# A two-layer graph network kernel: a seventh product split once more, additions begun from their addend, and one list schedule for every engine

## The chip, the cores and the metric

The kernel runs on one core of a Trainium2 chip. The metric is device time in microseconds (us), from the first to the last instruction of the core; the kernel before takes 1877.09 us, the median of three runs (1876.88 to 1878.52). A core has a matrix engine (TensorE, "PE" in the profile, with its weight loads as "PEld"), three engines for elementwise work (VectorE "DVE", ScalarE "ACT", GpSimd "POOL") and a queue of transfers (SyncE "SP"). Matmul results are in PSUM, eight banks of 128 x 512 float32; all else is in SBUF. Each engine works through its own list of instructions in the listed order and waits on semaphores for the others.

## The reference, cut to what matters

64 graphs of 256 nodes with 512 features, all float32. Two layers, each with a residual and a layer norm:

```python
# layer 0
deg = jnp.sum(adj, axis=-1, keepdims=True)
agg = jnp.einsum('bij,bjf->bif', adj, x) / jnp.maximum(deg, EPS)
out = relu(jnp.einsum('bnf,of->bno', jnp.concatenate([x, agg], axis=2), W))
x   = layernorm(x + out)
# layer 1
q, k = jnp.split(x @ Wqk, 2, axis=-1);  v = x @ Wv
agg  = jnp.einsum('bij,bjd->bid', adj, k * mask[:, :, None])
w    = inv_scale * mask * jnp.einsum('bid,bid->bi', q, agg)
x    = layernorm(x + softmax(w, axis=1)[:, :, None] * v)
```

The kernel moves matrices around the sums. In layer 0 it multiplies x with both halves of W first and lets adj act on the second result. In layer 1 it forms Wq Wk^T once, so that one product of x with [Wq Wk^T, Wv] (512 x 1024) gives what q and k give, and adj acts on x. So each layer of each graph is one 256 x 512 by 512 x 1024 product and one 256 x 256 by 256 x 512 product.

## The kernel before: the parts that count here

It works on **pairs** of graphs, 32 of them, and on layer 0 of pair j and layer 1 of pair j-1 in one round of its loop, so that each has work for TensorE while the other waits.

**The large product by Strassen (Winograd's form).** Both sides are cut into 2 x 2 blocks; seven block products P1 to P7 take the place of eight. Of these, P1, P2, P3 and P5 are cut once more and done by seven matmuls with 256 columns in place of eight. P4, P6 and P7 are done plainly, by four matmuls with 512 columns each for a pair.

```python
def inner(p, X, sides, w, q, done=lambda fifth: None):     # second step: 7 matmuls of 256 columns
    lo, hi = w[:, :HF], w[:, HF:]                          # two halves of a scratch bank
    def first_two():
        mm(hi, s(0), b["T1"], start=True)
        mm(lo, X.chunk(block, 0, 0), b["B11"])
        act.copy(q[0][:, :HF], lo)
        tick()
    def second():
        mm(lo, s(1), b["T2"])
        act.copy(q[0][:, HF:], lo)
        tick()
    def third():
        mm(lo, s(2), b["T3"])
        act.copy(q[1] ..., lo ... broadcast twice)         # cut
        fifth.append(small.tile([P, HF], F32, name="fifth", bufs=3))
        act.copy(fifth[0], hi)
        mm(q[0][:, :HF], X.chunk(block, 0, 1), b["B21"])
        tick()
    def last_two():
        mm(q[1][:, :HF], X.chunk(block, 1, 1), b["T4"])
        mm(q[0][:, HF:], s(3), b["B22"])
        if p in ("P1", "P5"):
            for k in range(2):
                vec.tensor_add(q[k][:, HF:], q[k][:, HF:], fifth[0])
        done(fifth[0])
        tick()

def outer(ps, k, X, slot, b, done=None):                   # plain: mm(ps[k], X.chunk(slot, k, e), b[:, e]), 512 columns
    ...
def pairs(ps, X, slot, b, done):
    return outer(ps, 0, X, slot, b, done) + outer(ps, 1, X, slot, b, done)
```

`s(r)` are sums of blocks of the left side ("xT_i", "x1T_i" in the profile; the outer sums are "xT_s", "x1T_s"), formed on GpSimd for every pair; the sums of the weights ("t", "t_i") are formed once, at the start. `q` are the two banks in which a product is accumulated onto the one before it; P6, P7 and P4 continue on P1's banks `u`.

**What happens to a finished product (layer 0; layer 1 is alike).**

```python
def after_p1(fifth):  act.copy(own[:, k, 0], u[k])                      # for k in 0, 1
def after_p2(fifth):  vec.tensor_add(own[:, k, 0], o[k], own[:, k, 0])  # for k in 0, 1
                      add_fifth(own[:, :, 0, HF:], fifth)
def after_p6(k):      act.copy(yt[:, k, 0], u[k]);  vec.tensor_add(yt[:, k, 0], y[k], yt[:, k, 0])
def after_p7(k):      act.copy(yt[:, k, 1], u[k]);  vec.tensor_add(yt[:, k, 1], y[k], yt[:, k, 1])
def after_p3(fifth):  vec.tensor_add(yt[:, k, 0], y[k], yt[:, k, 0])    # for k in 0, 1
                      add_fifth(yt[:, :, 0, HF:], fifth)
def after_p4(k):      act.copy(own[:, k, 1], u[k])
```

**The product with adj** (`gather`): seven matmuls of 256 columns for each graph, with adj's sums "sa" and the right side's sums "tv". In layer 0 the right half of the result goes into a tile `z`, and `norm0` adds z / deg to `own` later.

```python
def norm0(j):
    def scaled(k, t):
        vec.scalar_tensor_tensor(own[:, k, t, HF:], z[:, k, t], rdeg[:, k, t:t + 1], ..., op0=OP.mult, op1=OP.add)
    def residual(k, t, total):
        vec.scalar_tensor_tensor(o, o, 0.0, xs[j][:, k, t], op0=OP.max, op1=OP.add, accum_out=...)
```

**The order.** Every DVE, ACT and POOL instruction is issued through `InOrder.do`, which keeps program order (so the profile shows its line, L90, for nearly all of them), and every matmul through `mm` (L175). The side work that no product depends on at once (norms, masks, degrees, softmax) stands in queues; `tick()`, called after each step of a product, takes a step of a queue when a rough clock says that the engine is free. The order of the products is written by hand, in strings such as

```python
run("m p p", ...); fourth_sums(X, [0]); run("m p p m", ...); run("q q q", q=q); run("r q r m", ...); run("r s r", r=r, s=s)
run("s s j s a b", ...)                                    # s: P4 of layer 0; a to g: the product with adj
run("a n b q d q n c q e q n p g f", n=n, q=q, p=p, **g); b8(); run("p l p l p l", p=p, l=open1)
```

Of the kernel before, what the change touches and what calls it, by code (L numbers as in the profile page):

```python
# [2 lines left out]

# [6 lines left out]
F32 = mybir.dt.float32  # L36
# [5 lines left out]
P = 128  # L42
Q = 32
# [6 lines left out]

class Side:

    def __init__(self, pool, name, over, home=None):
        self.pool, self.name = pool, name
        self.slot = (0, 1, 2, over)
        home = pool.tile([P, 2 * N_SIDE], F32, name=name) if home is None else home
        self.a = home.rearrange("p (k u e v n) -> p k u e v n", k=2, u=2, e=2, v=2)
        self.s = self.i = None  # L60

    def open_sums(self):
        self.s = self.pool.tile([P, 2, 3, 2, P], F32, name=self.name + "_s")
        self.i = self.pool.tile([P, 4, 3, P], F32, name=self.name + "_i")

    def block(self, s, ks):
        return self.s[:, ks, self.slot[s]] if isinstance(s, int) else self.a[:, ks, s[0], :, s[1]]

    def chunk(self, s, k, e):
        return self.s[:, k, self.slot[s], e] if isinstance(s, int) else self.a[:, k, s[0], e, s[1]]  # L70

    def first_row(self, k, e):

        return self.a[:, k, :, e, 0]


class InOrder:

    def __init__(self, tc, engine, clock, cost):
        self.tc, self.engine, self.clock, self.cost, self.free = tc, engine, clock, cost, 0.0

    def __getattr__(self, name):
        def do(out, *args, **kwargs):
            size = 1
            for n in out.shape[1:]:
                size *= n
            self.free = max(self.free, self.clock[0]) + self.cost(name, size)
            return self.tc.keep_in_program_order(getattr(self.engine, name)(out, *args, **kwargs))  # L90
        return do
# [3 lines left out]
def resnorm_kernel(  # L95
# [22 lines left out]
    const = ctx.enter_context(tc.tile_pool(name="const", bufs=1))  # L118
    pool = ctx.enter_context(tc.tile_pool(name="pool", bufs=1))
    small = ctx.enter_context(tc.tile_pool(name="small", bufs=4))  # L120
    psum = ctx.enter_context(tc.tile_pool(name="psum", bufs=1, space=bass.MemoryType.PSUM))
    dram = ctx.enter_context(tc.tile_pool(name="dram", bufs=2, space=bass.MemoryType.DRAM))
    banks = [[psum.tile([P, F], F32, name=f"bank{2 * n + k}") for k in range(2)] for n in range(4)]

    (adjs, rows, xs, Xs, rdegs, sumsA, sumsM, owns, ys, zs, aggs, vs, x1Ts, scores, columns, rows_d, rows_w,
     probs) = ({} for _ in range(18))

    clock, chains, shared, quiet = [0.0], [], [1.0], [False]  # L130
    vec = InOrder(tc, nc.vector, clock, lambda name, n: shared[0] * ((0.17 if name == "bn_stats" else 0.07) + n / 960))
    act = InOrder(tc, nc.scalar, clock,
                  lambda name, n: 0.07 + n / 1200 if name == "copy" else (0.3 if n == F else 0.2) + n / 1000)
    gp = InOrder(tc, nc.gpsimd, clock, lambda name, n: 0.0)
    room = {vec: 0.6, act: 0.6}

    def queue(rank, name, *steps, ready=0.0):

        chains.append((rank, name, [ready], deque(steps)))
        chains.sort(key=lambda c: c[0])  # L140

    steady = []

    def step(chain):
        _, name, ready, steps = chain
        eng, work = steps.popleft()
        work()
        ready[0] = eng.free + (0.4 if eng is not vec else 0.7 if name == "norm" and len(steps) == NT else 2.2 if name == "finish" or name == "norm" and steady else 1.4) if steps and steps[0][0] is not eng else 0.0
        if not steps:
            chains.remove(chain)  # L150

    def tick():
        while not quiet[0]:
            for c in list(chains):
                if c[2][0] <= clock[0] and c[3][0][0].free <= clock[0] + room[c[3][0][0]]:
                    step(c)
                    break
            else:
                return

    def flush(*names):
        while True:
            c = next((c for c in chains if not names or c[1] in names), None)
            if not c:
                return
            step(c)

    def run(order, **units):
        for name in order.split():
            units[name].pop(0)()  # L170

    places, late_sums = [None], []

    def mm(ps, a, b, start=False):
        tc.keep_in_program_order(nc.tensor.matmul(ps, a, b, start=start, stop=True, skip_group_check=True))  # L175
        clock[0] += 0.86 if ps.shape[-1] == F else 0.43

    def first(out, in_):

        return tc.keep_in_program_order(nc.sync.dma_start(out, in_))  # L180

    send = first

    def load_adj(j):
        adjs[j] = pool.tile([P, 2, NT, N], F32, name="adj", bufs=2)
        for k in range(2):
            first(adjs[j][:, k], adj_t[2 * j + k].rearrange("(t p) i -> p t i", p=P))

    def load_rows(j):
        rows[j] = pool.tile([P, 2 * NT * F], F32, name="turn")[:, :2 * NT * N].rearrange(
            "p (k t n) -> p k t n", k=2, t=NT)
        for k in range(2):
            first(rows[j][:, k], adj[2 * j + k].rearrange("(t p) j -> p t j", p=P))

    def load_x(j):
        xs[j] = pool.tile([P, 2, NT, F], F32, name="x")
        for k in range(2):
            first(xs[j][:, k], x[2 * j + k].rearrange("(t p) f -> p t f", p=P))  # L200

    def load_xT(j, home=None):
        Xs[j] = Side(pool, "xT", S1, home)
        for k in range(2):
            first(Xs[j].a[:, k].rearrange("p h e t n -> p (h e) (t n)"),
                   x_t[2 * j + k].rearrange("(c p) n -> p c n", p=P))


    w0 = const.tile([P, 2 * NF, F], F32, name="w0")
    w1 = const.tile([P, 2 * NF, F], F32, name="w1")  # L210
    setup = ExitStack()
    sp = setup.enter_context(tc.tile_pool(name="setup", bufs=1))
    wqk = sp.tile([P, 2 * NA, F], F32, name="wqk")
    for a in range(NA):
        src = wqk_t.rearrange("(h a p) f -> a p h f", p=P, h=2)[a]
        first(wqk.rearrange("p (h a) f -> a p h f", h=2)[a], src)
    w0_of = w_t.rearrange("(k h p) o -> k p h o", p=P, h=H)
    for k in (0, 2):
        first(w0[:, k * H:(k + 1) * H, :], w0_of[k])
    load_xT(0)  # L220
    for k in (3, 1):
        first(w0[:, k * H:(k + 1) * H, :], w0_of[k])
# [3 lines left out]
    mask_sb = const.tile([P, B, NT], F32, name="mask_sb")  # L226
    first(mask_sb, mask_t)
    first(w1[:, NF:, :], wv.rearrange("(c p) o -> p c o", p=P))

    ident = const.tile([P, P], F32, name="ident")  # L230
    make_identity(nc, ident)
    eps = const.tile([P, 1], F32, name="eps")
    vec.memset(eps, LN_EPS)
    wide = [const.tile([P, Q], F32, name=f"wide{k}") for k in (0, 1)]
    for w in wide:
        vec.memset(w, 0.0)
    ones = const.tile([P, P], BF16, name="ones")
    vec.memset(ones, 1.0)

    def fill(pair):  # L240
        for k in range(2):
            mm(pair[k].rearrange("p (a n) -> p a n", n=P), ones,
               ones[:, None, :].to_broadcast([P, F // P, P]), start=True)
    for pair in (banks[0], *banks):
        fill(pair)

    def weight_product(c, ps):

        def unit(a):
            def go():  # L250
                mm(ps, wqk[:, a, c * P:(c + 1) * P], wqk[:, NA + a, :], start=(a == 0))
                if a == NA - 1:
                    act.copy(w1[:, c, :], ps)
                tick()
            return go
        return [unit(a) for a in range(NA)]

    def weight_sums(w, name):


        b11, b21, b12, b22 = (w[:, k * H:(k + 1) * H, :] for k in range(4))
        t1, t2, t4 = (const.tile([P, H, F], F32, name=f"{name}{k}") for k in (1, 2, 4))
        it = const.tile([P, 3, 4, HF], F32, name=f"{name}i")
        sides = {"T2": t2, "T3": b12, "T4": t4}
        sub = lambda *args: lambda: vec.tensor_sub(*args)

        def inner_of(n, p, b):
            c11, c12, c21, c22 = (b[:, e, h * HF:(h + 1) * HF] for e in range(2) for h in range(2))
            i1, i2, i4 = (it[:, r, n] for r in range(3))
            sides[p] = {"B11": c11, "B21": c21, "B22": c22, "T3": c12, "T1": i1, "T2": i2, "T4": i4}  # L270
            return [sub(i1, c12, c11), sub(i2, c22, i1), sub(c12, c22, c12), sub(i4, c21, i2)]
        work = ([sub(t1, b12, b11)] + inner_of(0, "P1", b11) + [sub(t2, b22, t1)] + inner_of(2, "P5", t1)
# [763 lines left out]
```

## Time and profile before

| What | Value |
|---|---|
| time, median of three | 1877.09 us |
| span of the profiled execution | 1877.0 us |
| PE busy, by its records | 1859.8 us in 7004 instructions |
| DVE, ACT, POOL busy | 1509.8, 1308.6, 910.1 us |
| mean granted TensorE clock | 0.998 |
| DMA, mean of the span | 97 GB/s, queue q1 35.8% of 16 engines |

How to read it: busy time is the time in which an engine worked on at least one instruction. Every float32 matmul stands in the trace as two records, and consecutive records overlap, so neither the sum of their lengths nor the busy share says how close TensorE is to its limit; the distance from one start to the next does. An idle stretch of an engine is put down to what it waited for ("released by"). The chain of waits follows the last instruction back, at each step to what released it.

### The profile page before, as it was taken

How to read it: one execution, taken by the hardware profiler on the slowest of the kernel's cores; microseconds unless marked ns; L12 is line 12 of the kernel's file. 1: busy time of each engine (PE TensorE's matmuls, PEld its weight loads, DVE VectorE, ACT ScalarE, POOL GpSimd, SP SyncE). 2: the span in 40 equal slices, each digit the busy share in tenths (PEclk: the TensorE clock that was granted, in tenths of full speed). 3: DMA queues.
4: the chain of work that ended last, by engine and by line, in shares of the span. 5: the costliest groups of instructions: out<-in, count | busy, mean ns of one | idle time of the engine just before them, and what ended most of it. 6: DMA issues, size and time to landing. Idle time of an engine off the chain costs nothing.

```text
span 1877.0 us, 25019 instructions
## 1 busy us (share of the span) xinstructions
PE 1859.8 (99%) x7004; PEld 1313.7 (70%) x7004; DVE 1509.8 (80%) x3180; ACT 1308.6 (70%) x3273; POOL 910.1 (48%) x1255
## 2 busy tenths in 40 slices
PE   9999999999999999999999999999999999999997
PEld 5667777767777677677677777776776776776765
DVE  6787888778888778887778887788877788877887
ACT  3667776677776677767777776777676777767766
POOL 4455453555444554535554545554455544355532
PEclk9999999999999999999999999999999999999999
DMA  6133334333333433343333334333434333333321
GB/s 225 57 74 80 100 92 118 86 96 94 104 97 91 112 83 99 90 119 85 98 91 105 96 97 107 85 97 93 115 85 106 87 101 96 99 105 85 97 61 58
DMA packets 380714, 181.27 MB, mean 97 GB/s; under 512 B 263712, under 2 KB 345248, under 8 KB 380576
## 3 DMA queue, kind: packets, MB, share of 16 engines
q1 hardware_dynamic: 380576, 179.67, 35.8%
q8 instruction: 57, 0.93, 0.2%
q14 instruction: 81, 0.66, 0.1%
HBM read 114.10 MB, written 34.06 MB: 79 GB/s over the span
## 4 chain that ended last, share of the span: by engine, by line
PE 95%; POOL 2%; issue 2%; ACT 1%; DVE 1%; POOLq 0%; DVEq 0%; ACTq 0%
PE bank L175 95%; POOL xT_i L90 1%; POOL xT_s L90 1%; POOL sa L90 0%; ACT own L90 0%; DVE own L90 0%; ACT x1T L90 0%; DVE v L90 0%; DVE bank L90 0%; ACT bank L90 0%; PE bank L629 0%; DVE st L90 0%; ACT adj L90 0%; DVE turn L90 0%; PE bank L652 0%
## 5 line engine op out<-in xcount | busy, mean ns | idle before, releaser
L90 ACT COPY bank<-bank 128x256 f32<-128x256 f32 (+1 forms) x768 | 332.4, 435 | 234.6 <-PE bank L175 223.6
L90 DVE TENSOR_TENSOR y<-bank,y 128x512 f32<-128x512 f32 x256 | 170.6, 686 | 133.1 <-ACT y L90 132.5
L90 ACT ACTIVATE own<-own,shift,rstd 128x512 f32<-128x512 f32 x254 | 199.0, 808 | 0.0
L90 POOL TENSOR_TENSOR x1T_s<-x1T,x1T_s 128x256 f32<-128x256 f32 x64 | 63.7, 1014 | 267.8 <-PE bank L175 267.8
L175 PE MATMUL bank<-tv,sa 128*128 128x256 f32 x768 | 192.5, 380 | 0.9 <-DVE tv L90 0.9
L90 POOL TENSOR_TENSOR x1T_i<-x1T_s 128x128 f32<-128x128 f32 x128 | 101.1, 790 | 183.5 <-DVE x1T_s L90 183.5
L90 ACT ACTIVATE junk<-own,less 128x512 bf16<-128x512 f32 x254 | 183.7, 723 | 3.0 <-DVE less L90 2.0
L175 PEld LDWEIGHTS bank<-tv,sa 128*128 128x128 f32 x768 | 145.4, 190 | 49.6 <-issue 22.9
L90 ACT COPY y<-bank 128x512 f32<-128x512 f32 x192 | 108.9, 583 | 95.2 <-PE bank L175 93.7
L90 POOL TENSOR_TENSOR sa<-adj 128x256 f32<-128x256 f32 x128 | 93.7, 732 | 166.6 <-DMA adj<-adj_t 152.8
L175 PE MATMUL bank<-w,x1T_s 128*128 128x512 f32 (+1 forms) x384 | 168.3, 521 | 0.0
L90 POOL TENSOR_TENSOR x1T_i<-x1T 128x256 f32<-128x256 f32 x64 | 55.1, 861 | 222.1 <-DMA x1T<-turn 209.4
L175 PE MATMUL bank<-t,xT_s 128*128 128x512 f32 (+1 forms) x384 | 159.6, 525 | 3.0 <-POOL sa L90 1.6
L90 DVE TENSOR_TENSOR v<-bank,v 128x512 f32<-128x512 f32 x186 | 119.2, 682 | 49.4 <-PE bank L175 49.4
L175 PE MATMUL bank<-t,x1T_s 128*128 128x512 f32 (+1 forms) x384 | 158.1, 521 | 0.3 <-ACT y L90 0.3
L175 PE MATMUL bank<-w,xT_s 128*128 128x512 f32 (+1 forms) x384 | 153.1, 521 | 0.0
L175 PE MATMUL bank<-t_i,xT_i 128*128 128x256 f32 x512 | 152.7, 380 | 0.3 <-POOL sa L90 0.2
L175 PE MATMUL bank<-t_i,x1T_i 128*128 128x256 f32 x512 | 152.2, 379 | 0.1
L175 PEld LDWEIGHTS bank<-t_i,x1T_i 128*128 128x128 f32 x512 | 97.1, 190 | 67.1 <-issue 49.5
L90 ACT COPY own<-bank 128x512 f32<-128x512 f32 x128 | 71.9, 587 | 91.8 <-PE bank L175 49.3
L175 PEld LDWEIGHTS bank<-t_i,xT_i 128*128 128x128 f32 x512 | 94.6, 189 | 58.2 <-issue 45.6
L175 PE MATMUL bank<-t,x1T 128*128 128x512 f32 x256 | 130.6, 592 | 0.0
(162 smaller groups left out, 4567.9 us busy)
## 6 DMA issues: line engine op xcount, KB each, us to landing
x<-x SPq DMA_DIRECT2D x64, 512.0 KB, 5.8
xT<-x_t SPq DMA_DIRECT2D x62, 512.0 KB, 5.6
out<-own SPq DMA_DIRECT2D x62, 512.0 KB, 3.2
x1T<-turn SPq DMA_DIRECT2D x480, 64.0 KB, 2.3
adj<-adj_t SPq DMA_DIRECT2D x64, 256.0 KB, 3.8
turn<-adj SPq DMA_DIRECT2D x64, 256.0 KB, 3.0
row<-d SPq DMA_DIRECT2D x31, 256.0 KB, 4.7
wqk<-wqk_t SPq DMA_DIRECT2D x4, 512.0 KB, 5.3
```

The source lines that it names most:

```text
L90: return self.tc.keep_in_program_order(getattr(self.engine, name)(out, *args, **kwargs))
L175: tc.keep_in_program_order(nc.tensor.matmul(ps, a, b, start=start, stop=True, skip_group_check=True))
```

## The change

Four things are changed.

1. **P4 of both layers is done by the second step too**, as P1, P2, P3 and P5 are: seven matmuls of 256 columns for four of 512. It accumulates onto banks that already hold P1, P6 and P7, so each of its four partial results is copied to SBUF by ACT and added to the bank by DVE. Its left side needs four sums more on GpSimd in each layer, its weights four more at the start. P6 and P7 stay plain.
2. **P2 and P3 begin from what they are added to.** The first contents of their banks are not a copy of a partial result but that partial result plus the tile that the product would be added to at its end (`onto`); the finished bank is then copied out by ACT, and the additions at the end and `add_fifth` go.
3. **No z.** In the product with adj of layer 0 every part is multiplied by 1/deg and added to `own` straight from its bank; the second product goes on in the bank c, which is started with a copy of the first.
4. **The order.** Nothing is issued while the program is walked through. Every instruction is recorded with its cost, its reads and writes; `Plan.latest` gives each a due date backwards from the order of the products, and `Plan.order` lists all engines by a simulated greedy schedule, in which each engine takes, of what can start soon, what is due first. Matmuls may change places too. The order of the products is a new one, one string for all rounds. Tiles are allocated once and used in rings.

The diff, cut to its core:

```diff
+INNER = ("P1", "P2", "P5", "P3", "P4")
+ORDER = ("L k k i i i L k k i m p p m p p q m q q q s r m s r r r a s b s d e J J c J J f K g K K K N H H "
+         "N Q A D H H Q Q C E Q N G N P P B P P F L L")
...
+    def order(self):
...
+                for s in ahead[e]:
+                    at = s.ready
+                    for b in s.banks:
+                        for other, end in last[b].items():
+                            if other != e:
+                                at = max(at, end + self.WAKE[e])
+                    if e == "PE" and at > free[e] - 0.15:
+                        at += 0.08
...
+                    soon = min(x[0] for x in found) + self.SLACK[e]
+                    pick = min((x for x in found if x[0] <= soon), key=lambda x: (x[2].due, x[0]))
...
-        def first_two():
-            mm(hi, s(0), b["T1"], start=True)
+        also = p in ("P4", "P6", "P7")
+        def common():
+            mm(hi, s(0), b["T1"], start=True)
+            if onto is not None:
+                vec.tensor_add(onto[:, :, HF:], twice(hi), onto[:, :, HF:])
+            else:
+                fifth.append(kept(hi))
+            if also:
+                for k in range(2):
+                    vec.tensor_add(q[k][:, HF:], q[k][:, HF:], fifth[0])
+        def first():
+            common()
             mm(lo, X.chunk(block, 0, 0), b["B11"])
-            act.copy(q[0][:, :HF], lo)
+            if also:
+                vec.tensor_add(q[0][:, :HF], q[0][:, :HF], kept(lo))
+            elif onto is not None:
+                vec.tensor_add(q[0][:, :HF], lo, onto[:, 0, :HF])
+            else:
+                act.copy(q[0][:, :HF], lo)
...
+        def third():
             mm(lo, s(2), b["T3"])
+            if also:
+                vec.tensor_add(halves(q[1]), halves(q[1]), twice(kept(lo)))
+            elif onto is not None:
+                vec.tensor_add(halves(q[1]), twice(lo), halves(onto[:, 1]))
+            else:
+                act.copy(q[1][:, :HF], lo)
+                vec.tensor_add(q[1][:, HF:], lo, fifth[0])
...
         def u1():
-            twice(u, "A11", "B11")
+            twice(u, "A11", "B11", True)
+            act.copy(c, u)
         def g5():
+            if own is not None:
+                onto(1, 1, p5)
+                onto(0, 1, p5)
         def u3():
+                onto(1, 1, u)
         def g3():
+                twice(c, "S4", "B22")
+                onto(0, 1, c)
...
-        def scaled(k, t):
-            o = own[:, k, t, HF:]
-            vec.scalar_tensor_tensor(o, z[:, k, t], rdeg[:, k, t:t + 1], o, op0=OP.mult, op1=OP.add)
...
+            "m": make("P2", pw[0], o, lambda k: act.copy(own[:, k, 0], o[k]), own[:, :, 0]),
+            "p": make("P6", pw[1], u, lambda k: vec.tensor_add(yt[:, k, 0], u[k], yt[:, k, 1])),
+            "q": make("P7", pw[0], u, lambda k: vec.tensor_add(yt[:, k, 1], u[k], yt[:, k, 1])),
+            "r": make("P3", pw[1], y, lambda k: act.copy(yt[:, k, 0], y[k]), yt[:, :, 0]),
+            "s": make("P4", pw[0], u, lambda k: act.copy(own[:, k, 1], u[k])),
...
-    for k in range(2):
-        mm(y[k][:, HF:], ident, held[0])
-    mm(y[1], ident, vs[j][1][:, 0])
```

In ORDER, lower-case letters are layer 0 (i P1, k P5, m P2, p P6, q P7, r P3, s P4, a to g the product with adj), capitals layer 1 (J P1, K P2, H P6, Q P7, N P5, P P4, L P3 of the pair before, A to G the product with adj).

## The prediction, written before the result was known

> **What bounds the kernel now.** I read the page's busy shares first, then the chain of waits:
>
> ```profile
> PE 1859.8 (99%) x7004; PEld 1313.7 (70%) x7004; DVE 1509.8 (80%) x3180; ACT 1308.6 (70%) x3273; POOL 910.1 (48%) x1255
> ...
> PE 95%; POOL 2%; issue 2%; ACT 1%; DVE 1%; POOLq 0%; DVEq 0%; ACTq 0%
> ```
>
> 95% of the chain that ended last is TensorE's own work, so TensorE is the bound. "99% busy" does not say how much of that is needed. The Trainium skill, "Perfetto Trace Analysis", section "Identifying the Most-Contended Engine", warns that matmul busy time is a poor measure of the distance to the limit because matmuls are pipelined. This trace agrees: a 256-column record lasts 379 ns in the mean, but the timeline of TensorE shows the next matmul starting much sooner (start, length, name, number of records; a matmul is two records):
>
> ```profile
> 921.35 0.59 PE L175 MATMUL bank<-t_i,xT_s 128*128 128x256 f32 x2
> 921.79 0.59 PE L175 MATMUL bank<-t,xT_i 128*128 128x256 f32 x2
> 922.22 0.59 PE L175 MATMUL bank<-t_i,xT_i 128*128 128x256 f32 x2
> 922.65 0.59 PE L175 MATMUL bank<-w,xT 128*128 128x256 f32 x2
> 923.35 1.95 PE L175 MATMUL bank<-t,xT_s 128*128 128x512 f32 x4
> 925.14 0.59 PE L175 MATMUL bank<-t_i,xT_i 128*128 128x256 f32 x2
> ```
>
> Here are both my unit costs and the look of a wait. 256-column matmuls start 0.43 us apart; over longer unbroken runs 0.4315. 512-column ones start 0.858 us apart (elsewhere 900.05, 900.91). From 922.65 the next should start at 923.08; it starts at 923.35: a wait of 0.27 us. From 923.35 two matmuls of 512 take 1.72, plus 0.07.
>
> So I count. A pair has in each layer 28 matmuls of 256 from the four inner products and 14 from the product with adj, and 12 of 512 (P4, P6, P7): in both layers 84 and 24. 84 x 0.4315 + 24 x 0.858 = **56.84 us**, if nothing waits. What a pair takes is the distance between equal places of the chain, cut by windows:
>
> ```profile
> core 0: us, PE busy (x) PEld busy (x) DVE busy (x) ACT busy (x) POOL busy (x), PEclk, DMA share, GB/s
> 751.55:808.72 57.17, 57.17 (x217) 40.85 (x218) 46.09 (x99) 40.87 (x103) 28.05 (x40) 1.00 0.37 97
> 808.72:865.90 57.18, 57.17 (x217) 40.51 (x215) 46.50 (x99) 40.49 (x103) 28.30 (x40) 1.00 0.37 97
> 865.90:923.10 57.20, 57.15 (x216) 40.65 (x216) 46.15 (x98) 40.47 (x103) 28.14 (x40) 1.00 0.37 98
> ```
>
> 57.2 against 56.84: a pair in the middle waits only some **0.36 us** in all. DVE is at 46.2 of 57.2 (81%), ACT at 71%, POOL at 49%. The whole span, by the timeline: 20.1 us to the first product (loads and Wq Wk^T), 32 x 56.84 = 1819, about 4.4 for transposes and the last additions on TensorE, 12 after its last product; that is 1855.5, which leaves some **21.5 us of waiting**: 30 x 0.36 = 11 in the middle, the rest in the first two pairs and the last (0.91 us at 46.7, 0.83 at 60.0, 0.79 at 77.7 and smaller ones).
>
> **What the change takes from TensorE.** P4 plain is 4 x 0.858 = 3.432 us, by the second step 7 x 0.4315 = 3.021: 0.412 us less. The Trainium skill, "TensorE: Matmul & The Clock Gate", section "Back-to-back issue gap", gives a matmul's cost as proportional to its columns plus about 2.5 ns. The trace agrees in kind: two 256-column matmuls cost 2 x 431.5 - 858 = 5 ns more than one of 512, so more, smaller matmuls lose little. There are 32 x 2 such products: 64 x 0.412 = **26.4 us**. A pair's floor is then 98 x 0.4315 + 16 x 0.858 = 56.02 us. At the end three small matmuls by the identity go; they partly lie in waits: 0.5 us. Nothing else in the change shortens TensorE's list.
>
> **What it does to the other engines, for a pair.** Durations are means of these rows of the groups:
>
> ```profile
> L90 DVE TENSOR_TENSOR y<-bank,y 128x512 f32<-128x512 f32 x256 | 170.6, 686 | 133.1 <-ACT y L90 132.5 <-PE bank L175 0.6
> L90 DVE TENSOR_TENSOR bank<-bank,fifth 128x256 f32<-128x256 f32 x256 | 94.2, 422 | 13.2 <-PE bank L175 13.0
> L90 DVE SCALAR_TENSOR_TENSOR own<-bank,rdeg,own 128x256 f32<-128x256 f32 x192 | 83.8, 478 | 17.6 <-PE bank L175 17.2
> L90 DVE SCALAR_TENSOR_TENSOR own<-z,rdeg,own 128x256 f32<-128x256 f32 x128 | 77.3, 604 | 0.0
> L90 DVE TENSOR_TENSOR y<-y,fifth 128x512 f32<-128x512 f32 x64 | 52.2, 815 | 7.0 <-ACT adj L90 0.5
> L90 ACT COPY bank<-bank 128x256 f32<-128x256 f32 x512 | 186.7, 365 | 197.5 <-PE bank L175 192.9 <-DVE y L90 2.3
> L90 POOL TENSOR_TENSOR xT_i<-xT_s 128x128 f32<-128x128 f32 x128 | 60.8, 475 | 2.4
> ```
>
> DVE loses: 8 adds into y, 6 into v, 2 into own, 2 into z and 3 into agg, all of 512 (21 x 0.685 = 14.4), the additions of "fifth" to SBUF tiles (2 x 0.815 + 0.935 + 2 x 0.549 = 3.7), 6 multiply-adds from a bank (2.9) and the 4 from z (2.4): 23.4 us. It gains: four adds for P6 and P7 in layer 0 (2.7), two of 1024 for P5 (about 1.2 each by doubling the 512 row less its fixed part, an estimate: 2.4), twelve multiply-adds from a bank (5.7), two adds into agg (1.4), for P2 and P3 of two layers 4 x (2 x 0.686 + 2 x 0.422) = 8.9, for the two P4 2 x (0.686 + 4 x 0.422) = 4.7: 25.8 us. Net **+2.4 us**. Neighbours overlap a little (two adds of 512 took 1.28 us together), so this is a ceiling: DVE goes from 46.2 to about 48 to 49 of 56.4, **86%**.
>
> ACT loses the copies of four inner products in each layer, 8 x (2 x 0.365 + 0.577 + 0.376) = 13.5 us, and gets 4 x 1.1 for P1 and P5, 8 x 0.37 for P4, six copies of 512 more for finished products and one in the products with adj (7 x 0.58): 11.5. Net -2 us. POOL gets 8 sums of 128 columns at 0.475 to 0.79 us: +5, to 33 of 56.4. None of the three becomes the bound by its sum.
>
> POOL and DVE hinder each other. The Trainium skill, "SBUF — State Buffer", section "Who interferes with whom", says that a DVE instruction with two SBUF inputs contends with a GpSimd instruction that reads SBUF. The trace agrees: own<-own,x of 512 takes 0.69 us at 57.07, where POOL is idle, and 0.927 in the mean. The change adds POOL work but removes DVE work of this kind (fifth, z: 9 instructions), so I take this as even.
>
> **Waits that may come.** P4's chain is new: TensorE writes the scratch half, ACT copies it, DVE adds it to the bank. The Trainium skill, "PSUM — Partial Sum Buffer", section "PSUM bank collisions raise a hardware error", has any two engines on one bank kept apart in time, so TensorE may not refill the scratch bank until ACT has left it. The trace before shows the same hand-over for P1 to P3, hidden by other products in between: TensorE's waits, by what released them, add up to little:
>
> ```profile
> PE bank L175 <- POOL sa L90: 1.8, 8, 0.2
> ...
> PE bank L175 <- ACT bank L90: 0.3, 1, 0.3
> ```
>
> P4 needs three such hand-overs, about 0.37 of ACT plus latencies each, so over a microsecond of other matmuls must stand between its steps. The new order gives them (s between a and b, P between B and F), and the schedule may pull later matmuls forward. Starting P2 and P3 from their addend saves work, but puts an SBUF tile that must be ready in front of a product.
>
> **Rivals.** (a) *The floor moves, waits stay*: 1877.1 - 26.4 - 0.5 = 1850. For it: two stalls a pair now, no engine above 90%. (b) *The schedule also takes waits out*: it can pull matmuls forward in the first and last pairs, where 10 us lie, and in the middle, where 11 do; all of that gone would be 1829, half 1840. Against it: the hand-made order already leaves 0.36 us of 57. (c) *New waits eat the gain*: every list is fixed beforehand from a cost model, DVE at 86% has less slack, and P4's chain passes three engines. One microsecond more of waiting a pair gives 1882. For it: DVE already waits for partners (132.5 us on ACT in the first row), so its work comes in bursts. (d) *DVE becomes the bound*: it would need over 57 us a pair, against 49; unlikely.
>
> **Range and chances.** I take (a) with 0.2 us more waiting a pair (+6) and 4 us less at the ends: 1850 + 2 = **1852 us**, a gain of 1.3%. The range is 1841 (half of the waits gone) to 1868 (0.5 us more a pair and nothing won at the ends). Faster by over 2% means below 1839.6, all of P4's gain and half the waits: 0.13. Slower by over 2%, above 1914.6, needs nearly 2 us of new waits a pair: 0.03. Within 2%: 0.84.
>
> **What would show it.** In the profile after: PE records 7004 + 2 x (6 x 32) less a few, about 7380; a steady pair of 56.2 to 56.6 us; DVE busy up to about 1560, ACT down to about 1245, POOL near 1060; no row with z. (b) would show as a pair at 56.0 and fewer gaps before 100 us; (c) as TensorE waits on ACT or DVE at P4's steps ("t_i" with xT or x1T) and a pair above 57. I am wrong if DVE's lists make TensorE wait in every pair, or if the start, whose order is wholly new, loses several microseconds.

## The result and the profile after

The changed kernel takes **1866.92 us** in the median (1866.57 to 1867.35), against 1876.99 before on the same chip; ratio 0.9946, 95% interval [0.9932, 0.996]. That is 10 us less. The forecast was 1852, a gain of 25: the time lies inside the range, but three fifths of the gain are missing.

The page of the kernel after, busy shares and the chain of waits by engine:

```profile
span 1865.2 us, 26366 instructions
PE 1834.0 (98%) x7382; PEld 1374.0 (74%) x7382; DVE 1595.6 (86%) x3511; ACT 1245.2 (67%) x3115; POOL 996.1 (53%) x1511
...
PE 83%; DVE 14%; issue 1%; ACT 1%; DMA 0%; SPq 0%; POOL 0%; ACTq 0%; DVEq 0%
```

The busy shares look as healthy as before. The last line does not: TensorE's share of the chain fell from 95% to 83%, and DVE's rose from 1% to 14%. Something on DVE now carries the end, though DVE is idle for 14% of the span. Cut at the start of one matmul that comes once in each pair (`bank<-t_i,x1T`, below), by windows:

```profile
core 0: us, PE busy (x) PEld busy (x) DVE busy (x) ACT busy (x) POOL busy (x), PEclk, DMA share, GB/s
888.82:945.51 56.69, 56.44 (x229) 42.60 (x229) 48.96 (x109) 38.62 (x98) 30.82 (x48) 1.00 0.36 98
945.51:1002.18 56.67, 56.42 (x229) 42.60 (x229) 49.18 (x109) 38.69 (x98) 30.75 (x48) 1.00 0.36 98
1002.18:1058.85 56.67, 56.42 (x229) 42.60 (x229) 49.38 (x109) 38.68 (x98) 30.76 (x48) 1.00 0.37 99
```

Most pairs in the middle now resemble each other to 0.02 us, so one late step in the pair comes back some 30 times. TensorE's waits, by what released them (us in total, times, longest), show it at once:

```profile
PE bank L355 <- DVE bank L270: 7.6, 30, 0.5
PE bank L355 <- DMA shared<-wqk_t: 2.8, 1, 2.8
```

I divided the two spans by the starts of the first product of layer 0 with adj (`bank<-y,adj`) in the timeline of TensorE, at pair 2 and at pair 31:

| Stage, us | before | after | difference |
|---|---|---|---|
| start, up to pair 2 | 137.9 | 134.8 | -3.2 |
| 29 pairs in the middle | 1660.8 (57.27 each) | 1645.4 (56.74 each) | -15.4 |
| last pair and end | 78.3 | 85.0 | +6.7 |

Each column is one execution. The differences add up to 11.9 us and not to 10.1, because the profiled execution of the kernel before was some 1.8 us longer than the median (a run's time is its span and 1.8 us, as 1867.0 and 1865.2 after). The lists of before, profiled once more in e9 below, give 136.7, 1659.7 and 78.3: the start and the middle are certain to about a microsecond, and the longer end is not in doubt.

Two things are wrong: the middle brings less than its 29 x 0.824 = 23.9 us of matmuls, and the end became longer.

**The late step.** The timeline of TensorE around one border of pairs (start, length, name, number of records, idle time before it):

```profile
944.66 0.59 PE L355 MATMUL bank<-own,adj 128*128 128x256 f32 x2
945.51 0.67 PE L355 MATMUL bank<-t_i,x1T 128*128 128x256 f32 x2 [0.25 <-DVE bank L270]
```

A 256-column matmul from 944.66 lets the next start at 945.09; it starts at 945.51, so **0.42 us** late (the 0.25 in brackets counts only from the modelled end of the one before). The bank that it refills is read by DVE's third addition of a product begun from its addend. The timeline of DVE at that place (L270 is one recording helper for all rows; go by the tiles):

```profile
943.05 0.68 DVE L270 TENSOR_TENSOR x1T<-x1T 128x512 f32<-128x512 f32 x1
943.65 0.72 DVE L270 TENSOR_SCALAR less<-sum 128x2 f32<-128x2 f32 x1
944.28 0.47 DVE L270 SCALAR_TENSOR_TENSOR own<-bank,rdeg,own 128x256 f32<-128x256 f32 x1
944.68 0.68 DVE L270 TENSOR_TENSOR bank<-bank,y 128x512 f32<-128x512 f32 x1
```

And the timeline of GpSimd beside it:

```profile
943.61 0.73 POOL L270 TENSOR_TENSOR x1T_s<-x1T,x1T_s 128x256 f32<-128x256 f32 x1 [0.77 <-PE bank L355]
```

DVE has no gap. `bank<-bank,y`, which TensorE waits for, starts at 944.68 because DVE was busy, and what kept it is the second line: an operation on **two numbers a partition**, the mean for the norm, that took 0.72 us. A GpSimd sum had started 0.04 us before it and ended at 944.34; `less` ended at 944.37. By tiles, `less` in the kernel before (count, shortest/median/longest in ns):

```profile
L90 DVE TENSOR_SCALAR less<-sum x126: 157/196/1109, 56.5 to 1850.4; 128x2 f32<-128x2 f32 x126
```

and in the kernel after, where its median has doubled:

```profile
L270 DVE TENSOR_SCALAR less<-sum x126: 138/400/722, 57.2 to 1851.2; 128x2 f32<-128x2 f32 x126
```

I matched every `less` in the timeline of after with GpSimd's, 128 with two of one number. The 39 that start with GpSimd idle take 0.13 to 0.17 us. The 89 that start while a GpSimd sum runs all end within 0.06 us of that sum's end. In the kernel before it is the same, 65 and 63 of 63. So the hold-up is old; it has become more frequent, and its place is new. The Trainium skill, "SBUF — State Buffer", section "Who interferes with whom", has an explanation: `tensor_scalar`, though not the form that also writes out its accumulator, can take a port pair that it shares with GpSimd, and then one blocks the other fully. These lengths, up to 0.72 us, agree; the trace shows who waits until when, not the port itself. The plan that makes the lists knows nothing of it: its cost table has, for fewer than 16 columns, `return 0.08, 0.158, both`, that is 0.08 us and no port.

### The profile page after: what moved, and what is told of

The parts are those of the page before. It is cut to its first block, busy times and chain, and to the rows that moved or that the text cites. A ratio compares the mean times of both kernels' runs of the same rounds, so it can differ in the third digit from the quotient of the medians.

```text
span 1865.2 us, 26366 instructions
## 1 busy us (share of the span) xinstructions
PE 1834.0 (98%) x7382; PEld 1374.0 (74%) x7382; DVE 1595.6 (86%) x3511; ACT 1245.2 (67%) x3115; POOL 996.1 (53%) x1511
## 4 chain that ended last, share of the span: by engine, by line
PE 83%; DVE 14%; issue 1%; ACT 1%; DMA 0%; SPq 0%; POOL 0%; ACTq 0%; DVEq 0%
PE bank L355 83%; DVE own L270 7%; DVE bank L270 3%; DVE less L270 1%; DVE y L270 1%; DVE x1T L270 1%; DMA shared<-wqk_t 0%; ACT junk L270 0%; DVE rdeg L270 0%; ACT own L270 0%; PE bank L361 0%; DVE turn L270 0%; DVE x L270 0%; DVE t_i L270 0%; ACT fifth L270 0%
## 5 line engine op out<-in xcount | busy, mean ns | idle before, releaser
L270 ACT COPY fifth<-bank 128x256 f32<-128x256 f32 x384 | 144.0, 376 | 302.0 <-PE bank L355 300.2
L270 POOL TENSOR_TENSOR x1T_i<-x1T 128x128 f32<-128x128 f32 (+1 forms) x128 | 81.0, 634 | 455.3 <-PE bank L355 315.8
L270 DVE TENSOR_TENSOR bank<-bank,fifth 128x256 f32<-128x256 f32 (+1 forms) x576 | 259.2, 456 | 44.1 <-PE bank L355 23.1
L270 ACT COPY shared<-bank 128x512 f32<-128x512 f32 x314 | 182.2, 582 | 66.1 <-PE bank L355 60.6
L355 PE MATMUL bank<-w,x1T 128*128 128x512 f32 (+1 forms) x512 | 206.5, 486 | 0.0
L270 ACT COPY bank<-bank 128x256 f32<-128x256 f32 (+1 forms) x352 | 145.4, 420 | 84.6 <-PE bank L355 74.2
L355 PE MATMUL bank<-w,xT 128*128 128x256 f32 (+1 forms) x496 | 200.0, 486 | 0.0
L270 ACT ACTIVATE junk<-own,less 128x512 bf16<-128x512 f32 x254 | 183.5, 723 | 21.0 <-DVE less L270 18.7
L270 DVE TENSOR_TENSOR y<-bank,y 128x512 f32<-128x512 f32 x192 | 132.2, 689 | 75.9 <-PE bank L355 72.1
L270 ACT ACTIVATE own<-own,shift,rstd 128x512 f32<-128x512 f32 x254 | 194.9, 824 | 2.8 <-DVE shift L270 2.6
L270 DVE TENSOR_TENSOR shared<-bank,shared 128x512 f32<-128x512 f32 (+1 forms) x157 | 137.6, 891 | 52.3 <-PE bank L355 52.0
L270 DVE SCALAR_TENSOR_TENSOR own<-bank,rdeg,own 128x256 f32<-128x256 f32 x384 | 174.8, 476 | 5.8 <-PE bank L355 1.9
L270 ACT COPY y<-bank 128x512 f32<-128x512 f32 x256 | 149.2, 585 | 45.1 <-PE bank L355 44.8
L270 ACT COPY own<-bank 128x512 f32<-128x512 f32 x192 | 112.5, 588 | 35.5 <-PE bank L355 35.1
```

The source lines that it names most:

```text
L270: self.plan.record(self.name, lambda: call(out, *args, **kwargs), outs, ins, busy, done, port)
L355: plan.record("PE", lambda: nc.tensor.matmul(ps, a, b, start=start, stop=True, skip_group_check=True), [ps], [a, b], busy, busy + 0.165, w ...
```

## The experiments

**e1: the same lists, `less` in the form with an accumulator**, a second output with the sum of its results, which nobody reads. All instructions stay in their places on all engines; only this differs:

```diff
-            vec.tensor_scalar(less, total, -1.0 / F, None, op0=OP.mult)
+            vec.tensor_scalar(less, total, -1.0 / F, 0.0, op0=OP.mult, op1=OP.add,
+                              accum_out=small("unused", [P, 1]))
```

> The changed kernel with every instruction in the same place; only the 128x2 multiplication that makes the negative mean ('less') also writes an accumulator, so that it should no longer be held up by GpSimd (0.40 us median in the changed kernel, up to 0.72). Theory (that held-up DVE instruction delays the add for which TensorE waits 0.42 us in each steady pair): 'less' falls to about 0.25 us, a steady pair from 56.67 to 56.3 us, the whole by 9 to 13 us to about 1856. Rival (DVE is simply full there, or the adds of P2 are too wide): the pair falls by less than 0.15 us and the whole by less than 5 us.

Measured: **1853.79 us**, 0.9874 [0.9857, 0.989] of before, 13 us less than the change as it was. `less` by its tile:

```profile
L270 DVE TENSOR_SCALAR_CACHE_REDUCE less<-sum x126: 124/149/156, 57.3 to 1837.9; 128x2 f32<-128x2 f32 x126
```

The form costs an accumulator read of about 0.08 us more, and yet none of the 126 takes longer than 156 ns. Two pairs by windows:

```profile
866.19:922.38 56.19, 56.19 (x230) 42.71 (x229) 48.93 (x113) 38.81 (x98) 31.21 (x48) 1.00 0.37 99
922.38:978.57 56.19, 56.19 (x230) 42.72 (x229) 48.70 (x113) 38.79 (x98) 31.82 (x49) 1.00 0.38 99
```

TensorE's waits on DVE's work in its banks:

```profile
PE bank L355 <- DVE bank L270: 0.9, 3, 0.5
```

And the chain of waits:

```profile
PE 97%; DVE 2%; ACT 1%; DMA 0%; issue 0%; SPq 0%; POOL 0%; ACTq 0%; DVEq 0%
```

DVE is almost as busy in a pair (48.8 us against 49.2), the periodic wait is gone, 97% of the chain is TensorE's, and a pair takes 56.19 us with a floor of 56.02. So this operation, and not DVE's load, took the time in the middle.

**e9: the same edit in the kernel before**, as a control.

> The kernel before, with the one edit that the kernel after had in e1: the operation that writes less also writes an accumulator that nobody reads. Theory (the long less is a cost of the new lists, where it stands next to a GpSimd sum and in front of an addition that a matmul waits for): in the old lists less lasts 196 ns in the median and no matmul waits behind it, so the median stays within 2 us of 1877. Rival (the small operation costs every kernel the same): it falls by some 10 us, to 1867, and the change then brings about 13 us of its own and not 23.

Measured: 1878.59 us, 1.0002 [0.9993, 1.0011] of before. `less`, by its tile, falls to a median of 154 ns, and nothing follows:

```profile
L90 DVE TENSOR_SCALAR_CACHE_REDUCE less<-sum x126: 138/154/157, 55.2 to 1848.2; 128x2 f32<-128x2 f32 x126
```

The lists are those of before, and in them the hold-up cost TensorE nothing that can be seen. It became a cost through the new lists.

**e3 and e8: P4 by the second step or plain**, with `less` as it was (e3) and in the accumulator form (e8), the lists made anew:

```diff
-INNER = ("P1", "P2", "P5", "P3", "P4")
+INNER = ("P1", "P2", "P5", "P3")
```

> The changed kernel with P4 of both layers plain again (four matmuls of 512), all else as changed. TensorE's floor for a pair goes back from 56.02 to 56.84 us, DVE loses about 3.8 us a pair. Theory (P4's additions to the banks fill DVE and bring the new waits): waits fall to 0.3 us, a pair takes 57.1 to 57.2 us and the whole is 1877 to 1880. Rival (the waits come from the list schedule and the other parts): a pair takes 57.4 to 57.5 us, the whole is 1886 to 1891.

> The changed kernel with the 'less' of e1_less_acc and with P4 of both layers plain. Floor of a pair 56.84 us. Theory (the held-up 'less' made the waits with P4 plain too, and P4 by the second step makes next to none of its own): a mean pair of 57.0 to 57.2 us, down from 57.48 in e3_p4_plain, the whole 1866 to 1872. Rival (with P4 plain the waits have another cause): a pair stays at 57.4 or more, the whole at 1876 or more.

Measured: 1878.65 us (1.0004 [0.9995, 1.0012]) and 1877.16 us (0.9994 [0.9985, 1.0002]). The 29 middle pairs take 57.48 and 57.40 us each. The page of e8, busy shares:

```profile
PE 1856.2 (99%) x6998; PEld 1308.1 (70%) x6998; DVE 1470.4 (78%) x3311; ACT 1160.9 (62%) x2859; POOL 923.9 (49%) x1255
```

e8 is a miss: its rival came, so with P4 plain the waits have another cause than `less`. In e3 the total fell where the theory had it, the pair where the rival had it. Without P4's new form the change is worth nothing that can be seen (e3): the new order, the starts from addends and the missing z together leave the time where it was. That zero is a sum. By stages:

| Stage, us | before | e3 | e8 | e1 |
|---|---|---|---|---|
| start, up to pair 2 | 137.9 | 131.8 | 131.5 | 135.0 |
| 29 pairs in the middle | 1660.8 | 1666.8 | 1664.5 | 1631.9 |
| last pair and end | 78.3 | 79.6 | 79.6 | 85.0 |

With P4 plain the start is 6 us shorter than before and the middle 4 to 6 us longer. P4's form brings 1878.65 - 1866.92 = 11.7 us with `less` in the way, but 1877.16 - 1853.79 = **23.4 us** with it out of the way. That this lies near the 26.4 worked out is chance. From e8 to e1 the middle gains 32.6 us, where 29 x 0.824 = 23.9 are P4's matmuls; the other 8.7 are waiting, which falls from 57.40 - 56.84 = 0.56 to 56.27 - 56.02 = 0.25 us a pair. The start and the end together lose 8.9. Lists differ within each of these pairs of kernels, so part of a difference may be theirs. With P4 plain, DVE is busy for 7 points less of the span, the pairs differ (56.3 to 58.5 us in e8), no wait comes back in each of them, and the accumulator form brings only 1.5 us.

**e10 and e11: two other ways around the collision.** e10 tells the cost table that this operation takes the port; e11 makes `less` on ACT. Both let the plan make new lists.

```diff
-            return 0.08, 0.158, both
+            return 0.08, 0.158, both or op == "tensor_scalar"
```
```diff
-            vec.tensor_scalar(less, total, -1.0 / F, None, op0=OP.mult)
+            act.activation(less, total, AF.Copy, scale=-1.0 / F)
```

> The kernel after, with less as it was and one word of the plan's cost table altered: the plan now takes less for an operation that holds the port shared with GpSimd, so it places it where it thinks GpSimd idle. Theory: the collision is one that a better table avoids; TensorE's periodic wait of 0.42 us a pair falls by half or more, and the median to 1855 to 1861. Rival: the plan's times are off by more than the 0.4 us that count, so placing less by them helps nothing: 1864 to 1869, with less still at a median near 0.4 us.

> The kernel after, with less made by ScalarE (a copy with a scale) and the lists made anew. It is another way to take the port collision out. Theory: a middle pair of 56.2 to 56.5 us and a median of 1854 to 1860. Rival (it was not the port but the place in DVE's list, or the accumulator form did something else): ScalarE's longer chain to the norms costs what DVE saves, 1863 to 1870.

Measured: 1890.81 us (1.0071 [1.0053, 1.0089]) and 1874.15 us (0.9979 [0.9971, 0.9987]). Both are misses for my theory as I put it. In e10 the median of `less` fell only to 272 ns, so the placing helped partly, and the remade lists make TensorE wait elsewhere. Its waits in e10:

```profile
PE bank L355 <- ACT bank L270: 9.8, 9, 1.2
PE bank L355 <- DVE bank L270: 6.7, 11, 0.7
```

e11 is the better lesson. Two neighbouring pairs by windows:

```profile
934.48:991.65 57.17, 56.63 (x230) 42.69 (x229) 46.36 (x104) 39.86 (x102) 30.85 (x46) 1.00 0.36 97
991.65:1047.84 56.19, 56.19 (x230) 42.58 (x228) 47.28 (x106) 39.18 (x102) 32.96 (x49) 1.00 0.39 99
```

and the first line of its waits of TensorE:

```profile
PE bank L355 <- ACT shared L270: 5.9, 13, 0.5
```

Nearly every second pair takes 56.19 us, as in e1, so the collision can be taken out in this way too. The pairs between have a new late step, a copy on ACT, and lose about 1 us; the start and the end together are 5.3 us longer than in e1. Remaking the lists is an experiment of its own: it changes more than what was edited. Only e1, with its lists held, isolates the cause.

**e2, e5, e6: the end.** In the timeline of ACT the norms of pair 30 stand at 1849.84 to 1853.2 right ahead of those of the last pair, at 1856.72. Pair 30's softmax had been put off until nothing else was left; from the last matmul to the end it takes 14.6 us (1850.6 to 1865.2), against 9.1 before (1867.9 to 1877.0). e2 gives the instructions of that softmax due dates 30 us earlier. e5 takes e1 and does the last pair's P4 of layer 1 plain, which spares its three hand-overs where little other work is left to hide them. e6 does both, and is e1 otherwise.

```diff
     def order(self):
         self.latest()
+        for s in self.hurry:          # what the last softmax(j - 1) recorded
+            s.due -= 30.0
```
```diff
-            "P": make("P4", w4, u, lambda k: dot(u[k], k, 1)),
+            "P": [w for k in range(2) for w in outer(u, k, Y, A22, W1["t4"], lambda k: dot(u[k], k, 1))]
+                 if plain4 else make("P4", w4, u, lambda k: dot(u[k], k, 1)),
```

> The changed kernel, with the due dates of the softmax of the last pair but one set 30 us earlier; all lists are the same up to the last 45 us. Theory (the tail is longer because this softmax is listed late and pushes the last pair's norms behind it): last matmul to the end falls from 14.6 us to about 9 to 10 us, the whole by 4 to 6 us to about 1862; steady pairs stay at 56.67. Rival (P4's chain at the very end makes the tail longer): less than 1.5 us.

> The kernel of e1_less_acc, with the P4 of layer 1 plain for the last pair alone (its weights are put back by one DVE subtraction); all lists before the last 60 us are the same. Theory (P4's copies and additions, which stand right in front of the last scores, lengthen the tail): from the last pair's first product with adj to the end 82 us or less in place of 85.0, the whole about 1850 to 1851. Rival (only the late softmax of the pair before counts): within 1 us of 1853.8.

> As e5_tail_p4, with the softmax of the pair before the last also due 30 us earlier. Theory (the two causes add): 79 to 81 us from the last pair's first product with adj to the end, the whole about 1848 to 1849. Rival (the hurried softmax only moves the wait to TensorE, as when done alone): no better than e5_tail_p4.

| us | median | middle, a pair | last pair and end |
|---|---|---|---|
| after | 1866.92 | 56.74 | 85.0 |
| e2, earlier softmax | 1865.96 | 56.73 | 82.9 |
| e1 | 1853.79 | 56.27 | 85.0 |
| e5, e1 with plain P4 at the end | 1852.34 | 56.28 | 83.3 |
| e6, e5 and earlier softmax | **1849.46** | 56.30 | 79.8 |
| before | 1876.99 | 57.27 | 78.3 |

e2 was a miss, and e5 fell short too: alone they move the median by 1.0 and 1.5 us. In e2 the end after the last matmul did shrink to 9.1 us, but the last matmul came 3.1 us later; among the waits of TensorE in e2 stands one that was 0.7 us long in after:

```profile
PE bank L792 <- DVE w L272: 2.2, 1, 2.2
```

Together (e6 against e1) they bring 4.3 us in the median and 5.2 at the end, more than 2.1 and 1.7 at the end one by one, and the wait for `w` is gone in e6. So each seems to have hidden part of the other. That is not firm: e5's four runs alone spread over 3.4 us, and the earlier softmax was not run with e1's `less` and P4 unchanged. e6 ends 9.1 us after its last matmul, as the kernel before does. At 0.9846 [0.9832, 0.9861] of before it is the fastest of all these kernels, and 17 us faster than the change as it was.

**e4 and e12: without the starts from addends.** P2 and P3 are begun with copies and added at the end, for instance

```diff
-lambda k: act.copy(own[:, k, 0], o[k]), own[:, :, 0]),
+lambda k: vec.tensor_add(own[:, k, 0], o[k], own[:, k, 0])),
```

> The changed kernel with P2 and P3 of both layers begun from copies again and added to their addend at the end; DVE's columns stay the same by count (1536 for each product either way), ACT gets 256 columns less. Theory (which operation stands on TensorE's path matters only through what holds DVE up): 1862 to 1872 us. Rival (beginning from the addend puts a 512-column DVE add between two matmuls of P2 and so makes the 0.42 us wait): 1850 to 1858 us. If beginning from the addend is a gain of its own: above 1875 us.

> The kernel of e1, without the part of the change that begins P2 and P3 from their addend (they are copied into their banks and added at the end, as in e4), and with the read of the softmax row brought forward in SyncE's list, so that it does not stand behind the transposed reads as in e4. Theory (beginning from the addend shortens DVE's work by some microseconds a pair and nothing on TensorE): the lists hold, a middle pair stays below 57 us, and the median is 1854 to 1872. Rival (without it DVE's list runs late wherever the row's read stands): as in e4, above 1900.

Measured: 1943.68 us (1.0348 [1.0333, 1.0364]) and 1914.05 us (1.0193 [1.0177, 1.0209]). The theory failed in both; of e12 the rival came, above 1900 us. In e4 the chain of waits shows a list at fault:

```profile
PE 65%; DVE 11%; SPq 8%; ACT 6%; DMA 6%; issue 2%; POOL 2%; DVEq 0%; ACTq 0%; POOLq 0%
```

8% is SyncE's queue: the read of the softmax row stands there, in most pairs, behind 15 or 16 issues for x1T, at about 0.67 us each. e12 brings that read forward and has e1's `less` besides, and the middle pair falls from 59.2 to 58.2 us, still 2 above e1. By the page, DVE is busy for 1594.3 us in e12 and for 1580.8 in e1, only 0.4 us a pair apart, so the starts from addends do not spare DVE several microseconds, as I had written. What the remaining 2 us are, I can't say: lists differ throughout, no single wait stands out (the longest sum is 12.7 us, on ACT's copies, which is 0.4 us a pair), and e10 and e11 show what remade lists can cost. The worth of this part of the change stays open.

**e7: matmuls in exactly the order of the string**, each tied to the one before, with e1's `less`:

```diff
         if engine == "PE":
+            if self.last_pe:
+                self.last_pe.next.append((step, False))
+                step.missing += 1
+            self.last_pe = step
             step.due = self.clock
```

> The kernel of e1_less_acc, but matmuls keep the order of the string; only the other engines are listed by due dates. Theory (P4's three hand-overs are hidden because matmuls change places): a steady pair goes from 56.19 to over 57.2 us and the whole above 1883. Rival (the order string hides them by itself): a pair below 56.6, the whole below 1868.

Measured: 2583.98 us, 1.3767 of before. TensorE is busy for 80% of the span and waits for the hand-overs, by the first lines of its waits:

```profile
PE bank L360 <- DVE bank L275: 136.6, 279, 1.2
PE bank L360 <- ACT fifth L275: 98.3, 126, 1.1
```

The string gives due dates, not an order. It is the moving of matmuls that hides the hand-overs, P4's among them.

## Why the prediction was half right

**Right.** TensorE is the bound, and two sizes of matmul give its time. What shows P4's saving is the pair and not the 23.4 us between e8 and e1: e1's steady pair, 56.19 us, lies below the 56.84 that the old count of matmuls needs, and within 0.17 of the new floor of 56.02. The records came to 7382, ACT to 1245.2 us. DVE rose by 3.0 us a pair, to 49.2, where I had a ceiling of 2.4; in e1, with the long `less` gone, by 2.6, its new accumulator reads included (my total of 1560 us for DVE was too low even for my own +2.4 in 32 pairs; 1595.6 were measured). DVE as the bound (d) did not come. One of my two signs of being wrong did: DVE's list made TensorE wait in every pair.

**Wrong: contention "taken as even".** I set POOL's extra work against the DVE instructions that go, and stopped. I looked only at instructions with two SBUF inputs, where the trace of before had an operation of another kind, `less` at 157 to 1109 ns for two columns. My allowance of 0.2 us more waiting a pair was close in size by accident: waiting grew from 57.27 - 56.84 = 0.43 to 56.74 - 56.02 = 0.72 us, by 0.29. But it has two parts of opposite sign. With `less` out of the way, e1's middle pair waits 56.27 - 56.02 = 0.25, so in these lists 0.18 of waiting did go, as rival (b) had it (with P4 plain, in e8, 0.13 came); `less` put back 0.47, as rival (c) had it. (a), that waits stay, describes neither. I had looked for (c) at P4's hand-overs; it came from an instruction that the change does not touch.

**Wrong: "4 us less at the ends".** This is the larger miss. The start gave 3.2 us and the end took 6.7, so 3.5 more instead of 4 less. The gap is wider still: the forecast had, on top of the 4, P4's saving in the three pairs outside the middle (2.5 us) and 0.5 for the last small matmuls, so it needed 7 less. I had counted waits that a schedule could remove, and none that it could add: the order of the last pair, where TensorE no longer has other products to hide what is put off. The stages of e8 and e1 show with what it came. With P4 plain, start and end together take 211.1 us against 216.2 before, 5.1 less, about the gain that I expected of the order. With P4 by the second step, in the lists made for it, they take 220.0: the start is 3.5 us longer, and the last matmul is followed by 14.6 us in place of 10.6. Why those lists lose at the start is open. e6 wins back 5.2 of the 6.7 at the end; the other 1.5 I haven't explained, but 1.3 of it is there with P4 plain too (79.6 against 78.3).

**Too high:** POOL, set at +5 us a pair, rose by 2.6 (28.2 to 30.8). Nothing in the argument rests on it.

e1's 1853.8 us lies next to my 1852, and that is not the forecast coming true. It has 5 us more gained in the middle than the bare count of matmuls gives, and the longer end still in it.

## What to carry to other kernels

When a list is fixed beforehand, look, tile by tile, for small operations whose longest time is many times their shortest, and see what runs beside them: an idle share of 14% on an engine does not help the one instruction that is late. Change such an instruction with the lists held, since a remade list brings late steps of its own. And cut a span into start, middle and end before judging a schedule: gains of a steady pair can be lost at the ends, and a total near the forecast can be the sum of two differences of opposite sign.

## What the hardware showed

A DVE `tensor_scalar` on 128 x 2 numbers took 0.13 to 0.17 us beside an idle GpSimd and up to 0.72 us beside a running one in the kernel after (1.11 in the kernel before), ending with GpSimd's instruction in all 89 cases of the kernel after. With an accumulator as second output the same work never took longer than 157 ns (156 in e1, 157 in e9), plus about 80 ns for the read of the accumulator. Smaller did not mean safer. `shift`, a product of two such tiles in SBUF, is held up too, but not always. Of its 128 in e1, by tile,

```profile
L270 DVE TENSOR_TENSOR shift<-less,rstd x128: 148/160/702, 61.3 to 1845.8; 128x2 f32<-128x2 f32 x126, 128x1 f32<-128x1 f32 x2
```

86 start beside a running GpSimd sum. 59 of these end within 0.06 us of that sum's end; all of them started 0.08 us or more after the sum had. 26 started within 0.02 us of the sum's start and took about 0.15 us, as beside an idle GpSimd (the last started just before its sum ended). In this trace it counts which of the two came first.
